# A four-layer graph network on Trainium2: in the last three layers the first block's neighbours past the 15th share one transfer

## The chip, the cores and the metric

The kernel runs on one core of a Trainium2 chip. The core has five engines with a queue each, which they take in order: TensorE (PE in the profile; PEld is its weight load), VectorE (DVE), ScalarE (ACT), GpSimd (POOL) and SyncE (SP). They wait for one another through semaphores. Plain transfers are started from SP's queue, indirect ones (a list of row numbers picks the rows) from POOL's. The metric is the device time of one execution in microseconds; a lower one is better. It is given as the median of ten runs; the profile is of one execution more.

## The reference

4096 nodes with 256 features pass four attention layers over one sparse graph. Each layer normalises, applies a weight matrix, and gives each node a softmax-weighted sum over its neighbours and itself:

```python
# layer 0
h = jnp.maximum(_layernorm(x, axis=-1), 0.0)
x = x + _L0_gnn_ref(h, adj, L0_gnn_W, L0_gnn_a)
# layers 1, 2, 3: the same with _L1_gnn_ref, _L2_gnn_ref, _L3_gnn_ref
...
# L0, and L2 with a bias and without elu: 4 heads, scores from two vectors
e = s_i[:, None, :] + s_j[None, :, :]
e = jax.nn.leaky_relu(e, negative_slope=0.2)
e = jnp.where((adj == 0)[:, :, None], -jnp.inf, e)
alpha = jax.nn.softmax(e, axis=1)
out = jnp.einsum('ijh,jhd->ihd', alpha, Wh).reshape(n, heads * d)
...
# L1: 1 head, sums the nodes rather than their products
att = jax.nn.softmax(e, axis=1)
return h + att @ node
...
# L3: dot products, 4 heads of 64
scores = jnp.einsum('hnd,hmd->hnm', q, k) / np.sqrt(HEAD_DIM)
attn = jax.nn.softmax(scores + mask[None, :, :], axis=-1)
ctx = jnp.einsum('hnm,hmd->hnd', attn, v)
```

The graph is drawn at random and symmetric, with some 8 neighbours a node.

## The kernel before

A first stage (to about 430 us) reads the 4096 x 4096 adjacency, makes a list of at most 23 neighbours for each node, computes layer 0's table and part of its sums, and sorts the nodes by their number of neighbours, most first. Each node's row is then written to its place in that order. A flag checks the lists' limits; when it fails, a dense path runs instead (it doesn't here).

The layers then work on 32 **blocks** of 128 nodes, one node to a partition. As the nodes are sorted, block b needs only `CAPS[b]` columns of neighbours: 23 for block 0, then 14, 13, 12, 12, down to 3 for block 31. A row with fewer neighbours has its list filled with the number n = 4096, the table's one extra row, whose scores are so low that their share is 0. Layers 1 to 3 take the blocks in the order 0, 31, 1, 30, 2, 29 and so on (`ORDER`).

For layer l, each block writes its 128 rows to a table in HBM, `s_tab`. Rows are 264 floats wide in layers 0 and 2, 288 in layer 1 (with the node's own list in the last columns) and 512 (key and value) in layer 3. When the last rows of a table have landed, the next layer starts:

- `layer` goes over the blocks; `fill` issues the transfers ahead of use. One neighbour column of one block is one indirect transfer from POOL (`fetch`, L757): 128 rows, one to a partition, into one **slot** of a ring in SBUF. The ring has 18432 floats a partition: 69 slots in layer 2, 64 in layer 1, 36 in layer 3. A block takes consecutive slots (in layers 2 and 3 one more where its count is odd) and starts over at slot 0 where the end doesn't fit; `fill` stops as long as the slots belong to a block that is not yet done in program order. A transfer into a slot that was used waits, on the chip, for its last reader.
- `scores` makes the scores of a block's columns and of the node itself. In layers 1 and 2 that is one addition over all columns (L918); in layer 3 a product with the node's query and a sum over each head, for 8 columns at a time (L937, L940). `mutual` checks in layer 1 that each neighbour lists the node too (L965 to L973), and ACT takes the neighbours' places in the new order from the rows (L924), so that layers 2 and 3 gather by place. Then come the maximum, the difference and the exponential (L949, L950, L957).
- `weigh` normalises and sums. In layer 1 DVE multiplies and adds column by column (L1010). In layers 2 and 3 DVE multiplies 8 columns at a time by their shares (L1039), and PE adds them up in PSUM, two slots to a product with the identity (L1044); the node's own term is either one of the slots (odd counts) or a product of its own (L1032).
- `settle` adds the sums to x (L1078; in layer 3 L1068 and L1069, into `s_out`, of which there are three), normalises, and `turned`, `times` and `advance` make the next layer's rows (L742, L744, L750, L1091 to L1118). In layer 3 the outputs are stored by indirect transfers from POOL (`send`, L767), between the gathers.

The order of the layers' instructions is the order in which the program is written; each engine takes its own in that order. `reload`, ahead of layer 0, loads the sorted lists (`s_near`) and the rows (`s_rx`). PE's small results go through `pp`, a pool of three PSUM buffers. `verdict` gathers the flags at the end.

Of the kernel before, what the change touches and what calls it, by code (L numbers as in the profile page):

```python
# [19 lines left out]
P = 128  # L20
D = 256
# [20 lines left out]
    8, 8, 8, 7, 7, 7, 7, 6, 6, 6, 6, 5, 5, 5, 4, 3,  # L42
]

MARK = 8192.0
FAR = -1e30
W = 264
# [22 lines left out]


class Sparse:

# [611 lines left out]
    def reload(self):  # L687

        nc, tc, nt, n = self.nc, self.tc, self.nt, self.n
        by_place = self.placed.rearrange("(b p) k -> p b k", p=P)  # L690
        near = self.near = self.big.tile([P, nt, 32], U32, name="s_near")
        for a, b in ((0, 2), (nt - 2, nt), (2, nt - 2)):
            back = nc.sync.dma_start(
                out=near[:, a:b, 0 : TOPK + 1],
                in_=by_place[:, a:b, OWN : OWN + TOPK + 1].bitcast(U32),
            )
            if a == 0:
                for i in self.sent:
                    tc.add_manual_dep(
                        back.ins, i.name,  # L700
                        mybir.DependencyInfo(
                            mybir.DependencyClass.Sync, mybir.DependencyReason.DATA
                        ),
                        reason="every row",
                    )
            for k in {0: [], nt - 2: FIRST[:5], 2: FIRST[5:]}[a]:
                nc.sync.dma_start(out=self.rx[k], in_=self.placed[ts(k, P), 0:OWN])

        self.own_f = self.big.tile([P, nt], F32, name="s_own_f")
        nc.vector.tensor_copy(self.own_f, near[:, :, TOPK])  # L710

        where = self.big.tile([P, nt], F32, name="s_place_of")
        nc.gpsimd.iota(
            where, pattern=[[P, nt]], base=0, channel_multiplier=1,
            allow_small_or_imprecise_dtypes=True,
        )
        nc.vector.tensor_copy(near[:, :, TOPK - 1], where)
        self.away = self.big.tile([P, nt, TOPK], F32, name="s_away")
        nc.vector.tensor_scalar(
            self.away, near[:, :, 0:TOPK], float(n), FAR, ALU.is_ge, ALU.mult  # L720
        )

# [52 lines left out]
    def layers(self):  # L777
        tc, nc, nt = self.tc, self.nc, self.nt
        with ExitStack() as ctx:
            big = self.big = ctx.enter_context(tc.tile_pool(name="s_big", bufs=1))  # L780
            self.pool = ctx.enter_context(tc.tile_pool(name="s_main", bufs=2))
            self.pacc = ctx.enter_context(tc.tile_pool(name="s_pacc", bufs=4, space=PSUM))
            shares = ctx.enter_context(tc.tile_pool(name="s_pe", bufs=1, space=PSUM))
            self.pp = ctx.enter_context(tc.tile_pool(name="s_pp", bufs=3, space=PSUM))

            self.turns = 0
            self.shares = shares.tile([P, IB], F32, name="s_shares")

            rx = big.tile([P, nt, D + WL], F32, name="s_rx")
            self.x = [rx[:, b, 0:D] for b in range(nt)]  # L790
            self.rows = [rx[:, b, D : D + W] for b in range(nt)]
            self.rx = [rx[:, b, 0:OWN] for b in range(nt)]
            self.before = [rx[:, b, OWN - 4 : OWN] for b in range(nt)]
            self.listed = [rx[:, b, D : D + WL] for b in range(nt)]
            self.ring = big.tile([P, RING], F32, name="s_ring")
            self.eself = big.tile([P, nt, 4], F32, name="s_eself")
            self.norms = big.tile([P, 2, nt], F32, name="s_norms")
            self.both = big.tile([P, nt], F32, name="s_both")
            with tc.manual_schedule():
                self.reload()  # L800
                for l in range(4):
                    self.layer(l)
            return self.verdict()

    def slots(self, l, b):
        return max(CAPS[b] - EARLY, 0) if l == 0 else CAPS[b]

    def layer(self, l):

# [9 lines left out]
        def fill(i):  # L819
            nonlocal at  # L820
            while todo and nt - len(todo) <= i + AHEAD:
                j = todo[0]
                K = self.slots(l, j)

                room = K + (K % 2 if l > 1 else 0)
                s = (at if at + room <= slots else 0) if K else 0
                if any(s < e and b < s + room for b, e in held.values()) or (
                    l == 3 and len(held) > 3
                ):
                    return  # L830
                todo.pop(0)
                if l == 3:
                    vs[j] = self.pool.tile([P, D], F32, name=f"s_vself_{j}", tag="vself", bufs=5)
                    nc.sync.dma_start(out=vs[j], in_=self.tab[3][ts(j, P), D:])
                k0 = EARLY if l == 0 else 0
                for k in range(K):
                    at_k = self.near[:, j, k0 + k : k0 + k + 1]
                    self.fetch(ring[:, s + k, :], self.tab[l], at_k)
                held[j] = (s, s + room)
                at = s + room if K else at  # L840

# [29 lines left out]
        for i in range(nt):  # L871
# [3 lines left out]
                settle(c, (0,))  # L875
            norm(d)
            g = ring[:, held[b][0] : held[b][1], :]
            p = self.scores(l, b, self.rows[b], g[:, : self.slots(l, b), :])
            third(e)
            if l == 0:  # L880
                settle(c, (1,))
# [22 lines left out]
    def scores(self, l, b, mine, g):  # L904
# [1 line left out]

        nc, pool = self.nc, self.pool
        H = 1 if l == 1 else 4
        K = self.slots(l, b)
        if K == 0:  # L910
            return None
        e = pool.tile([P, TOPK, H], F32, name=f"s_e_{l}_{b}", tag="e", bufs=3)
# [1 line left out]
        if l < 3:  # L914
            src = mine[:, D + H : D + 2 * H]
            if l > 0:
                nc.vector.tensor_tensor(e[:, K, :], mine[:, D : D + H], src, ALU.add)
            nc.vector.tensor_tensor(  # L918
                e[:, :K, :], g[:, :, D : D + H], src.unsqueeze(1).to_broadcast([P, K, H]), ALU.add
            )  # L920
            if l == 1:
                self.mutual(b, g)

                nc.scalar.copy(self.near[:, b, 0:K], g[:, :, WL - 1])  # L924
            slope = 0.01 if l == 1 else 0.2
            el = ek if l > 0 else ek[:, : K * H]
            nc.vector.scalar_tensor_tensor(el, el, slope, el, ALU.mult, ALU.max)
# [2 lines left out]
        else:  # L930
            q = self.shares[:, IB - D :]
            nc.scalar.copy(q, mine[:, 0:D])
            nc.scalar.copy(e[:, K, :], self.eself[:, b, :])
            for k0 in range(0, K, AT_ONCE):
                m = min(AT_ONCE, K - k0)
                kq = g[:, k0 : k0 + m, 0:D]
                nc.vector.tensor_tensor(  # L937
                    kq, kq, q.unsqueeze(1).to_broadcast([P, m, D]), ALU.mult
                )
                nc.vector.tensor_reduce(  # L940
                    e[:, k0 : k0 + m, :], kq.rearrange("p k (h d) -> p k h d", h=4), AX.X, ALU.add
                )
            nc.vector.tensor_tensor(
                e[:, :K, :], e[:, :K, :],
                self.away[:, b, :K].unsqueeze(2).to_broadcast([P, K, 4]), ALU.add,
            )
        by_head = e[:, : K + 1, :].rearrange("p k h -> p h k")
        top = pool.tile([P, H], F32, name=f"s_m_{l}_{b}", tag="m", bufs=3)
        nc.vector.tensor_reduce(top, by_head, AX.X, ALU.max)  # L949
# [10 lines left out]
    def mutual(self, b, g):  # L960

        nc, pool = self.nc, self.pool
        K = CAPS[b]
        eq = pool.tile([P, CAPS[0], TOPK - 1], BF16, name=f"s_eq_{b}", tag="eq", bufs=1)
        nc.vector.tensor_scalar(  # L965
            eq[:, :K, :], g[:, :, W : WL - 1], self.own_f[:, b : b + 1], None, ALU.is_equal
        )
        has = pool.tile([P, CAPS[0]], F32, name=f"s_has_{b}", tag="has", bufs=1)
        nc.vector.tensor_reduce(has[:, :K], eq[:, :K, :], AX.X, ALU.max)
# [5 lines left out]
    def weigh(self, l, b, me, g, p):  # L975

        nc, pool = self.nc, self.pool
        H = 1 if l == 1 else 4
        K = self.slots(l, b)
        tot = pool.tile([P, H], F32, name=f"s_t_{l}_{b}", tag="t", bufs=3)  # L980
        if K == 0:

# [22 lines left out]
        acc = both[:, 0, :]  # L1005
        self.turns += 1
        if l == 1:
            nc.vector.tensor_scalar(acc, me, p[:, K, :], None, ALU.mult)
            for k in range(K):
                nc.vector.scalar_tensor_tensor(  # L1010
                    acc, g[:, k, 0:D], p[:, k, :], acc, ALU.mult, ALU.add
                )
            return acc
        v0 = 0 if l < 3 else D


        pairs = l > 1
        full = pairs and K % 2 == 0
        if pairs and not full:
            mev = g[:, K, v0 : v0 + D]  # L1020
        else:
            mev = pool.tile([P, D], F32, name=f"s_me_{l}_{b}", tag="me", bufs=4)
        if full:
# [7 lines left out]
        elif full:  # L1031
# [1 line left out]
                both, lhsT=self.ident, rhs=mev.unsqueeze(1).to_broadcast([P, 2, D]),  # L1033
                start=True, stop=False,
            )
        for k0 in range(0, K, AT_ONCE):
            m = min(AT_ONCE, K - k0)
            v = g[:, k0 : k0 + m, v0 : v0 + D].rearrange("p k (h d) -> p k h d", h=H)
            nc.vector.tensor_tensor(  # L1039
                v, v, p[:, k0 : k0 + m, :].unsqueeze(3).to_broadcast([P, m, H, D // H]), ALU.mult  # L1040
# [1 line left out]
            for k in range(k0, k0 + m, 2 if pairs else 1):  # L1042
                if pairs:
                    nc.tensor.matmul(  # L1044
                        both, lhsT=self.ident, rhs=g[:, k : k + 2, v0 : v0 + D],
                        start=(k == 0 and not full), stop=(k + 2 >= K),
                    )
                else:
                    nc.tensor.matmul(  # L1049
                        acc, lhsT=self.ident, rhs=g[:, k, v0 : v0 + D],  # L1050
                        start=False, stop=(k + 1 == K),
                    )
        return both if pairs else acc

    def settle(self, l, b, acc, made):
# [631 lines left out]
```

## Time and profile before

| | us |
|---|---|
| median of 10 runs (1813.22 to 1820.92) | 1816.24 |
| the profiled execution | 1817.75 |
| its span | 1816.0 |
| layer 1, first gather to the next layer's first (642.05 to 1012.56) | 370.5 |
| layer 2 (1012.56 to 1388.4) | 375.8 |
| layer 3 (1388.4 to the span's end) | 427.6 |

Busy shares of the span: DVE 76%, POOL 65%, PE 54% (with matmul ends that are modelled), ACT 23%. POOL issues 924 gathers into the ring (`s_ring<-s_tab,s_near`), 277 in each of layers 1 to 3. A row of the timeline gives the start in us, the duration, the engine, the line, the operation, output and inputs, and in brackets the idle time before it with what ended it. A row of waits gives who waited for whom, the total in us, how often, and the longest. PEclk is the clock granted to TensorE as a share of the full one.

### The profile page before, as it was taken

The numbers are of one execution on the slowest core, as the hardware profiler recorded it, in microseconds if no ns is written. First come the engines' busy times: TensorE is split into PE (matmuls) and PEld (weight loads), VectorE is DVE, ScalarE is ACT, GpSimd is POOL, SyncE is SP. The second block draws the span as 40 slices with busy tenths as digits, with TensorE's granted clock in tenths as the row PEclk, the third lists the DMA queues.
The fourth block names the chain that finished last, engine by engine and source line by source line (L and its number), as shares of the span: only waits on it lengthen the run. The fifth ranks groups of instructions, "written<-read, shape, count | busy, mean of one in ns | idle before, by whom it ended". The sixth has DMA issues, their size and how long they took to land.

```text
span 1816.0 us, 14325 instructions
## 1 busy us (share of the span) xinstructions
PE 975.2 (54%) x2534; PEld 473.0 (26%) x2551; DVE 1383.4 (76%) x3900; ACT 424.5 (23%) x1240; POOL 1184.7 (65%) x1324
## 2 busy tenths in 40 slices
PE   4967787752676602222222067788684354454445
PEld 3623233220454401111111033334332121111112
DVE  6899989951689818888888167888885587887776
ACT  5864434101244401111111012222221000000000
POOL 1067756676666267777776577777773577776774
PEclk9989889875788955555555588899987677677787
DMA  9899877347633144444444344444443577665763
GB/s 323 280 393 361 293 271 254 101 144 235 191 96 95 45 104 124 132 129 133 131 132 112 76 121 133 132 137 131 136 131 120 155 213 209 207 208 180 210 204 109
DMA packets 123017, 312.89 MB, mean 172 GB/s; under 512 B 31236, under 2 KB 49671, under 8 KB 122920
## 3 DMA queue, kind: packets, MB, share of 16 engines
q0 software_dynamic: 68064, 207.46, 40.6%
q1 hardware_dynamic: 54856, 104.44, 16.3%
q14 instruction: 73, 0.60, 0.1%
q8 instruction: 24, 0.39, 0.1%
HBM read 276.80 MB, written 35.00 MB: 172 GB/s over the span
## 4 chain that ended last, share of the span: by engine, by line
DVE 38%; POOL 16%; DMA 15%; issue 14%; PE 14%; ACT 3%; DVEq 0%; SPq 0%; POOLq 0%; another core or an unknown queue 0%; ACTq 0%
DMA s_ring<-s_tab,s_near 10%; POOL s_ring L757 10%; DVE s_acc L1010 7%; PE s_acc L1044 5%; POOL s_g L757 4%; DVE s_cand L485 3%; DVE s_ring L1039 3%; PE s_ps_kv L750 2%; DVE s_g L549 2%; DVE s_ring L937 1%; DVE s_st L571 1%; PE s_ae L558 1%; PE s_acc L1049 1%; DVE s_e L940 1%; DMA out_dram<-s_out,s_near 1%
## 5 line engine op out<-in xcount | busy, mean ns | idle before, releaser
L757 POOL DMA_INDIRECT s_ring<-s_tab,s_near x924 | 883.3, 956 | 348.3 <-issue 185.6
L1044 PE MATMUL s_acc<-s_ring,s_ident 128*128 128x512 f32 x588 | 307.5, 675 | 187.6 <-issue 96.2
L757 POOL DMA_INDIRECT s_g<-s_tab,s_keep x192 | 183.1, 954 | 64.4 <-issue 56.1
L1044 PEld LDWEIGHTS s_acc<-s_ring,s_ident 128*128 128x128 f32 x588 | 125.8, 220 | 362.6 <-issue 241.1
L485 DVE MAX8 s_cand<-s_pt 128x8 f32<-128x256 f32 x512 | 181.4, 415 | 16.3 <-PE s_pt L483 15.7
L1039 DVE TENSOR_TENSOR s_ring<-s_ring,s_shares 128x2048 f32<-128x2048 f32 (+7 forms) x121 | 187.5, 1573 | 0.0
L742 PE MATMUL s_pht<-s_ident,s_h 128*128 128x128 f32 x128 | 34.3, 361 | 249.9 <-ACT s_h L734 249.9
L750 PE MATMUL s_ps<-s_we_l,s_ht 128*128 128x264 f32 x256 | 114.8, 592 | 93.0 <-ACT s_ht L744 93.0
L1010 DVE SCALAR_TENSOR_TENSOR s_acc<-s_ring,s_p,s_acc 128x256 f32<-128x256 f32 x277 | 135.7, 490 | 9.7
L263 ACT ACTIVATE s_low<-s_raw 128x1024 fp8e4<-128x1024 int32 x128 | 134.3, 1051 | 20.4 <-DMA s_raw<-in_adj_dram 18.6
L558 PE MATMUL s_ae<-s_g,s_ident 128*128 128x512 f32 x192 | 114.3, 691 | 38.0 <-DVE s_g L549 37.7
L478 PE MATMUL s_pt<-s_low,s_mark 128*128 128x512 fp8e4 x256 | 107.1, 418 | 34.2 <-DVE s_cand L485 13.8
L750 PE MATMUL s_ps_kv<-s_wkv,s_ht 128*128 128x512 f32 x128 | 83.6, 788 | 67.1 <-ACT s_ht L744 67.1
L577 ACT ACTIVATE s_y<-s_mv,s_eps 128x1 f32<-128x1 f32 x96 | 28.3, 294 | 388.8 <-DVE s_mv L572 388.8
L937 DVE TENSOR_TENSOR s_ring<-s_ring,s_shares 128x2048 f32<-128x2048 f32 (+7 forms) x48 | 81.1, 1690 | 35.3 <-DMA s_ring<-s_tab,s_near 34.7
L957 ACT ACTIVATE s_shares<-s_e 128x32 f32<-128x32 f32 (+8 forms) x87 | 17.6, 202 | 377.5 <-DVE s_e L950 377.5
L918 DVE TENSOR_TENSOR s_e<-s_ring,s_rx 128x8 f32<-128x8 f32 (+12 forms) x87 | 15.8, 181 | 116.1 <-DMA s_ring<-s_tab,s_near 110.8
L483 PE MATMUL s_pt<-s_places,s_stands 128*128 128x512 bf16 x239 | 98.9, 414 | 1.4 <-DVE s_stands L455 1.4
L750 PEld LDWEIGHTS s_ps<-s_we_l,s_ht 128*128 128x128 f32 x256 | 63.9, 276 | 124.1 <-ACT s_ht L744 114.1
L742 PEld LDWEIGHTS s_pht<-s_ident,s_h 128*128 128x128 f32 x128 | 18.0, 172 | 290.9 <-ACT s_h L734 278.8
L940 DVE TENSOR_REDUCE s_e<-s_ring 128x32 f32<-128x2048 f32 (+7 forms) x48 | 81.2, 1692 | 1.6
L502 POOL TENSOR_SCALAR s_ids<-s_top 128x23 f32<-128x23 f32 x32 | 10.1, 314 | 107.5 <-DVE s_top L493 107.1
(195 smaller groups left out, 1692.3 us busy)
## 6 DMA issues: line engine op xcount, KB each, us to landing
s_raw<-in_adj_dram SPq DMA_DIRECT2D x128, 512.0 KB, 7.9
s_ring<-s_tab,s_near POOLq DMA_INDIRECT x924, 3.0
s_rx<-s_placed SPq DMA_DIRECT2D x32, 262.0 KB, 7.3
s_tab<-s_kv SPq DMA_DIRECT2D x32, 256.0 KB, 2.9
s_tab<-s_keep SPq DMA_DIRECT2D x8, 528.0 KB, 6.8
s_tab<-s_rx SPq DMA_DIRECT2D x32, 132.0 KB, 2.4
s_keep<-in_x_dram SPq DMA_DIRECT2D x8, 512.0 KB, 8.7
s_vself<-s_tab SPq DMA_DIRECT2D x32, 128.0 KB, 3.0
```

Source lines behind the costliest of these rows:

```text
L263: nc.scalar.activation(low[r][:, ts(h, n // 4)], raw.pop(q), AF.Copy, saturate=False, accum_out=self.sums[:, r, h : h + 1],)
L478: nc.tensor.matmul(pt, lhsT=self.mark, rhs=lo[:, ts(g, IB)], start=True, stop=False)
L483: nc.tensor.matmul(pt, lhsT=self.stands[:, g, :], rhs=self.places, start=False, stop=True)
L485: nc.vector.max(out=cand[:, g * (IB // CH) + k, :], in_=pt[:, ts(k, CH)])
L558: nc.tensor.matmul(acc, lhsT=self.ident, rhs=g[:, :, k, 0:D], start=False, stop=(k == E - 1))
L750: self.nc.tensor.matmul(ps[:, :width], lhsT=ht[:, c, :], rhs=w[:, c, :], start=(c == 0), stop=(c == KC - 1),)
L757: return self.nc.gpsimd.indirect_dma_start(out=out, out_offset=None, in_=table[:, :], in_offset=bass.IndirectOffsetOnAxis(ap=idx, axis=0),)
L937: nc.vector.tensor_tensor(kq, kq, q.unsqueeze(1).to_broadcast([P, m, D]), ALU.mult)
L940: nc.vector.tensor_reduce(e[:, k0 : k0 + m, :], kq.rearrange("p k (h d) -> p k h d", h=4), AX.X, ALU.add)
L1010: nc.vector.scalar_tensor_tensor(acc, g[:, k, 0:D], p[:, k, :], acc, ALU.mult, ALU.add)
L1039: nc.vector.tensor_tensor(v, v, p[:, k0 : k0 + m, :].unsqueeze(3).to_broadcast([P, m, H, D // H]), ALU.mult)
L1044: nc.tensor.matmul(both, lhsT=self.ident, rhs=g[:, k : k + 2, v0 : v0 + D], start=(k == 0 and not full), stop=(k + 2 >= K),)
```

## The change

Block 0's lists are cut to 15 columns (`KEPT`) in layers 1 to 3. The entries past the 15th of all its rows, real neighbours only, are numbered through as **edges**, and one transfer fetches them, one edge to a partition. It goes to slot 16 of the block's room, which is now 17 slots in each of the three layers (before: 23 in layer 1, 24 in 2 and 3). The last column of the lists, and with it the number of columns in the softmax, stays 23.

`share_place`, called at the end of `reload`, makes two 0/1 matrices of 128 x 128 (row to edge, edge to row), the list of the edges' rows, and a check that there are at most 128. `more_scores` brings each edge its node's score or query by a product, computes the edge's score, and brings it back to its row and column by another. `more_rows` brings each edge its share, multiplies the fetched row by it, and a last product with `to_row` adds the edges' rows to their nodes: in layers 2 and 3 into the block's sum in PSUM, in layer 1 into a buffer that is added to x.

```diff
+KEPT = 15
+MORE = CAPS[0] - KEPT
...
+    def share_place(self):
+        near = self.near[:, 0, KEPT : CAPS[0]]
+        nc.vector.tensor_scalar(some, near, float(n), None, ALU.is_lt)
+        for k, by in ((0, (self.ones, self.below)), (1, (self.ones,))):
+            for lhsT in by:
+                nc.tensor.matmul(
+                    ps[:, ts(k, MORE)], lhsT=lhsT, rhs=some, start=(lhsT is self.ones),
+                    stop=(lhsT is by[-1]),
+                )
...
+        nc.vector.scalar_tensor_tensor(self.to_edge, i, many, past, ALU.is_lt, ALU.mult)
+        nc.tensor.transpose(pt[:, 0:P], self.to_edge, self.ident)
+        nc.scalar.copy(self.to_row, pt[:, 0:P])
+        nc.tensor.matmul(pe[:, : MORE + 4], lhsT=self.to_edge, rhs=of, start=True, stop=True)
...
+        nc.vector.scalar_tensor_tensor(self.far, self.none, float(n), row, ALU.mult, ALU.add)
+
+    def more_scores(self, l, mine, ge, e):
+        if l < 3:
+            nc.tensor.matmul(
+                ps[:, 0:H], lhsT=self.to_edge, rhs=mine[:, D + H : D + 2 * H], start=True,
+                stop=True,
+            )
+            nc.vector.tensor_tensor(s, ge[:, D : D + H], ps[:, 0:H], ALU.add)
+        else:
+            nc.tensor.matmul(ps[:, 0:D], lhsT=self.to_edge, rhs=mine[:, 0:D], start=True, stop=True)
+            nc.vector.tensor_tensor(ge[:, 0:D], ge[:, 0:D], ps[:, 0:D], ALU.mult)
+            nc.vector.tensor_reduce(
+                s, ge[:, 0:D].rearrange("p (h d) -> p h d", h=H), AX.X, ALU.add
+            )
...
+        nc.vector.tensor_tensor(
+            to, self.which.unsqueeze(2).to_broadcast([P, MORE, H]),
+            s.unsqueeze(1).to_broadcast([P, MORE, H]), ALU.mult,
+        )
...
+        nc.tensor.matmul(back, lhsT=self.to_row, rhs=to, start=True, stop=True)
+        nc.vector.tensor_tensor(
+            e[:, KEPT : CAPS[0], :], back,
+            self.away[:, 0, KEPT : CAPS[0]].unsqueeze(2).to_broadcast([P, MORE, H]), ALU.add,
+        )
+
+    def more_rows(self, l, p, ge):
+        nc.scalar.copy(own, p[:, KEPT : CAPS[0], :])
+        nc.tensor.matmul(ps, lhsT=self.to_edge, rhs=own, start=True, stop=True)
+        nc.vector.tensor_tensor(
+            to, ps, which.unsqueeze(2).to_broadcast([P, MORE, H]), ALU.mult
+        )
+        nc.vector.tensor_reduce(s, to.rearrange("p j h -> p h j"), AX.X, ALU.add)
+        nc.vector.tensor_tensor(v, v, s.unsqueeze(2).to_broadcast([P, H, D // H]), ALU.mult)
+        return ge[:, v0 : v0 + D]
...
     def slots(self, l, b):
-        return max(CAPS[b] - EARLY, 0) if l == 0 else CAPS[b]
+        return max(CAPS[b] - EARLY, 0) if l == 0 else min(CAPS[b], KEPT)
...
-                room = K + (K % 2 if l > 1 else 0)
+                more = l > 0 and j == 0
+                room = KEPT + 2 if more else K + (K % 2 if l > 1 else 0)
...
                     self.fetch(ring[:, s + k, :], self.tab[l], at_k)
+                if more:
+                    self.fetch(ring[:, s + KEPT + 1, :], self.tab[l], self.far)
...
+            if more:
+                self.more_scores(l, mine, g[:, KEPT + 1, :], e)
...
         if l == 1:
+            if more:
+                rows = self.more_rows(l, p, g[:, KEPT + 1, :])
+                by_edge = self.pp.tile([P, IB], F32, tag="ps", name="s_by_edge")[:, 0:D]
+                nc.tensor.matmul(by_edge, lhsT=self.to_row, rhs=rows, start=True, stop=True)
             nc.vector.tensor_scalar(acc, me, p[:, K, :], None, ALU.mult)
...
+            if more:
+                nc.vector.tensor_tensor(self.x[b], self.x[b], by_edge, ALU.add)
             return acc
...
+        if more:
+            rows = self.more_rows(l, p, g[:, KEPT + 1, :])
+            nc.tensor.matmul(
+                both, lhsT=self.to_row, rhs=rows.unsqueeze(1).to_broadcast([P, 2, D]),
+                start=False, stop=True,
+            )
```

In layer 1 `more_scores` also does the list check for the edges (four small instructions on DVE) and takes the edges' places into `self.far` (ACT), by which layers 2 and 3 fetch. In layers 2 and 3 `more_rows` comes after the last columns' L1039, and its small product after their L1044 in PE's queue. `share_place` has 18 instructions on DVE, three iotas on POOL, five products on PE and a copy on ACT.

## The prediction

> **What bounds the kernel now.** I read the stage windows first, then each engine's waits inside a stage, then the timeline at the layer starts. Layers are l = 0 to 3, times are span microseconds. The windows' columns are PE, PEld, DVE, ACT, POOL busy, granted clock, DMA share, GB/s.
>
> ```profile
> 638.00:676.00 38.00, 0.00 (x0) 0.00 (x0) 0.45 (x4) 0.48 (x3) 26.74 (x28) 0.50 0.49 100
> 676.00:996.00 320.00, 84.46 (x180) 43.90 (x180) 278.14 (x951) 50.87 (x185) 238.17 (x250) 0.50 0.47 129
> ...
> 1012.00:1046.00 34.00, 0.00 (x0) 0.00 (x0) 0.08 (x1) 0.00 (x0) 25.52 (x27) 0.50 0.51 96
> 1046.00:1364.00 318.00, 247.92 (x599) 119.78 (x600) 257.11 (x750) 76.22 (x262) 239.66 (x251) 0.90 0.48 131
> ```
>
> l = 1 and l = 2 each open with some 35 us in which only POOL works: it issues the 23 gathers of block 0. A gather costs POOL 0.95 us and 0.30 us to the next, a pitch of 1.257 us, and POOL then issues without a gap: 250 in 320 us is 1.27 each. Who is late at the end of a layer is in the timeline:
>
> ```profile
> 669.76 0.95 POOL L757 DMA_INDIRECT s_ring<-s_tab,s_near  x1 [0.30 <-issue]
> 675.85 0.19 DVE L918 TENSOR_TENSOR s_e<-s_ring,s_rx 128x23 f32<-128x23 f32 x1 [37.55 <-DMA s_ring<-s_tab,s_near]
> ...
> 989.15 0.95 POOL L757 DMA_INDIRECT s_ring<-s_tab,s_near  x1 [0.30 <-issue]
> 995.91 0.17 DVE L918 TENSOR_TENSOR s_e<-s_ring,s_rx 128x8 f32<-128x8 f32 x1
> ...
> 1207.86 0.95 POOL L757 DMA_INDIRECT s_ring<-s_tab,s_near  x1 [0.30 <-issue]
> 1211.01 0.20 DVE L918 TENSOR_TENSOR s_e<-s_ring,s_rx 128x40 f32<-128x40 f32 x1 [1.21 <-DMA s_ring<-s_tab,s_near]
> ...
> 1360.89 0.95 POOL L757 DMA_INDIRECT s_ring<-s_tab,s_near  x1 [0.30 <-issue]
> 1364.43 0.19 DVE L918 TENSOR_TENSOR s_e<-s_ring,s_rx 128x32 f32<-128x32 f32 x1 [0.98 <-DMA s_ring<-s_tab,s_near]
> ```
>
> A waiting DVE starts 3.15 us after a block's last gather (1207.86 to 1211.01). In l = 2 it still waits at the last block (3.54): POOL bounds l = 2. In l = 1 it starts 6.76 late and without a wait: after block 0, DVE bounds l = 1, with POOL 3.6 us behind it as the next bound. Block 0 is special: its last gather takes 6.09 us to DVE's start (5.7 in l = 2, 6.3 in l = 3). Of block 0's 128 rows only 46, 21, 9, 7, 2, 0, 0, 0 have a neighbour in columns 16 to 23 (counted from the reference's adjacency); the rest fetch the one pad row. That this makes them late is my reading; the lateness is in the rows.
>
> In l = 3 the scores are taken 8 columns at a time while gathers land, and the ring has only 36 slots of this width:
>
> ```profile
> 1401.07 2.29 DVE L937 TENSOR_TENSOR s_ring<-s_ring,s_shares 128x2048 f32<-128x2048 f32 x1 [10.99 <-DMA s_ring<-s_tab,s_near]
> ...
> 1422.41 2.02 DVE L937 TENSOR_TENSOR s_ring<-s_ring,s_shares 128x1792 f32<-128x1792 f32 x1 [6.50 <-DMA s_ring<-s_tab,s_near]
> ...
> 1431.70 14.62 PE L1044 MATMUL s_acc<-s_ring,s_ident 128*128 128x512 f32 x28 [42.87 <-DVE s_ring L1039]
> ...
> 1434.05 0.95 POOL L757 DMA_INDIRECT s_ring<-s_tab,s_near  x1 [13.24 <-PE s_acc L1044]
> ...
> 1446.58 2.29 DVE L937 TENSOR_TENSOR s_ring<-s_ring,s_shares 128x2048 f32<-128x2048 f32 x1 [1.06 <-DMA s_ring<-s_tab,s_near]
> ```
>
> Blocks 0, 31 and 1 want 24 + 4 + 14 = 42 slots, so block 1 starts over at slot 0 and POOL stands 13.24 us until block 0's first products have read it. From there POOL issues 268 transfers (gathers and output stores) in 343 us with only two gaps over 1 us (3.46 and 2.61), and DVE's largest wait is for stores that POOL issues late:
>
> ```profile
> DVE s_out L1068 <- DMA out_dram<-s_out,s_near: 34.6, 12, 7.9
> ```
>
> So POOL bounds l = 3 as well, after one hole of 13 us.
>
> **l = 1.** POOL: 23 gathers become 16, 7 x 1.257 = 8.8 us. DVE waits for column 15 instead of 23, at 642.05 + 14 x 1.257 + 3.15 = 662.8 instead of 675.85: 13.0 earlier. The shared transfer lands 1.26 later, behind the list check (L965 to L973, some 2 us), so nobody waits. DVE loses 8 multiply-adds (23 took 12.04, so 0.523 each: 4.2) and a third of L965 and L969 (0.4). It gains about ten instructions: eight small ones at a pitch of 0.21 (as L970, L973) and two over 256 columns at 0.42 (as L1078), 2.5 us. And it now stands twice for PE: at "back", and at the shares in more_rows, which go over ACT (0.25). The nearest trip there and back is L734 to L742 to L744 at this layer's clock: ACT done at 695.06, ACT again at 696.01, 0.95 us for two products. Bounds: 0.7 (one such product alone) and 2.6 (the four of L750, 2.13, with their waits); I take 1.2, a small product with weights of its own being nearest to L742. Net: 2.5 + 2.65 - 4.6 = +0.6. DVE could be 12.4 earlier; POOL allows 8.8 plus what the lag can shrink, from its smallest, 6.2 us at block 14, to 3.15: **11.9 us**.
>
> Trainium skill, "DMA: Bandwidth & Descriptors", section "Anatomy of one DMA": a GpSimd transfer takes about 2.0 us plus its bytes over 436 GB/s, whatever rows it reads; an estimate of 2.3 us for these 147 KB. By it DVE would start only 8 x 1.257 = 10.1 us earlier, l = 1 would gain 9.5, and the sum below would be 2.4 us less. The trace disagrees: 6.09 against 3.15 for the same bytes.
>
> **l = 2.** Gathers: **8.8 us**. DVE starts 12.6 earlier, and loses 2.1 (L1039 over 15 columns is 2.29 + 2.02, not 6.41). It pays 0.6 and 1.2 in more_scores. In more_rows it stands behind PE, which takes its queue in order: 16 product instructions (28 took 13.84; five at 0.85, then 0.43) are 9.0 us, 2.0 of it under the second L1039, so 7.0 of wait, then 0.7 for the small product and 0.8 of DVE's own. Net +8.2, so DVE is 4.4 ahead of the old trace where POOL is 8.8 ahead. The 4.4 is covered: DVE's old 5.04 us wait for those same products (L1078, block 0) mostly goes, and it waits 24.8 us for gathers later in the layer. Without that cover l = 2 would gain 4.4.
>
> **l = 3.** The rooms are 17 + 4 + 14 = 35: block 1 fits, and POOL runs through to 1428.7. Block 30 then takes slots 0 to 3 from 1430. Are they read by then? DVE: chunk one as before to 1405.7, chunk two (7 columns, from 1410) to 1414.1, more_scores 2.5, softmax as before, first L1039 done near 1421.7; the products of slots 0 to 3, two cold pairs, near 1425.3. Yes, with 4.7 us to spare. Block 2 takes slots 4 to 16, the last free after more_rows near 1434, wanted at 1450; block 29 wants 18 to 22 from 1452.7, where block 1 (DVE at 1438.5) frees 21 and 22 near 1454, after the three before them are issued. So the wait goes and doesn't come back: 12.9 us (13.24 less the usual 0.30), with 8.8 for the gathers **21.7 us**. DVE is behind POOL for a while: more_rows makes it wait 7 again, block 1 starts at 1438.5 instead of 1446.58, block 30 at 1453.8 (1465.6), block 2 at 1460.6 (1472.4), 11.8 ahead. It recovers the other 9.9 from the 34.6 us that it used to wait for stores.
>
> **share_place.** 18 small DVE instructions at 0.21 and two PE trips: 6.5 us (4 to 12 by the bounds of the trip), ahead of l = 0. DVE later idles 12.42 us there:
>
> ```profile
> 461.80 0.23 DVE L918 TENSOR_TENSOR s_e<-s_ring,s_rx 128x68 f32<-128x68 f32 x1 [12.42 <-DMA s_ring<-s_tab,s_near]
> ```
>
> That hides it; bare, it would cost its 6.5. POOL's three iotas (0.16 for 32 columns, 0.56 for 512) fall into the 1.80 us before its first gather. The verdict's transposes, now issued at 1388, draw on the same three PSUM buffers as the new products and may be pushed into or behind l = 3; their chain is 2.1 us long. I take 0.5 us for all of this (0 to 4).
>
> Trainium skill, "SBUF — State Buffer", section "SBUF: two separate sides": a vector copy in a two-port mode locks GpSimd out of the port through which it writes descriptors. By that rule the new small instructions, some 10 us of them, could hold gathers back, at worst for all of it, and the sum would be 1784. The trace has 924 gathers of 949, 953 and 1199 ns (least, median, most) beside a busy DVE, so I charge nothing.
>
> **Sum.** 11.9 + 8.8 + 21.7 - 0.5 = 41.9 us. Span 1816.0 to 1774.1; this execution took 1817.75 in all, so about 1775.9; the median shown is 1816.24, 1.5 below, which puts it at 1774.3. **1774**, main case 1768 to 1781.
>
> **Rivals.**
> (B) The ring wait moves rather than goes: block 30 or 29 meets slots not yet read. For it: 36 slots, four blocks held. Against: the walk, with 1 to 5 us of room. l = 3 then keeps 8.8: 29 us, **1787**.
> (C) DVE never recovers: trips nearer 2.6, and more_rows' wait at the cold 0.85 throughout. For it: DVE is at 278 of 320 in l = 1. Against: its waits in l = 2 and l = 3. Gains 11.9 + 4.4 + 11.8 = 28: **1788**.
> (D) The openings were hidden anyway: **1816**. Against: 37.55 and 35.8 us of idle DVE, released by the gathers.
> (E) Slower: DVE's in-order stand behind PE in more_rows is what ends each layer, and the earlier start buys nothing. Price: 6.5 + 0.6 + 8.2 + 4.3 (l = 3: 11.0 added, 6.7 removed), 19.6 us, **1836**. It decides once the stand exceeds the 12 to 13 us of earlier start; I count 7.
>
> More than 128 shared edges would send the program down its dense path; the reference's adjacency gives 85.
>
> **Chances.** Main 0.71, B 0.11, C 0.10, D 0.02, E 0.06. B and C make the upper end, 1789; the lower, 1766, is no overhead at all with the two POOL gaps of 3.46 and 2.61 gone too. A difference under 0.2% can't be told from none here; faster 0.92, same 0.02, slower 0.06.
>
> **What would show it.** Right: L918 of l = 1 some 20.7 us after the layer's first gather (33.8 now); no POOL gap over 2 us between l = 3's first and 50th gather; DVE idle about 7 us in more_rows at l = 2 and 3, and DVE's L918 still waiting for gathers at the end of l = 2. Wrong: a POOL gap there, or l = 2's last block starting far over 3.5 us after its gather.

## The result, and the profile after

The changed kernel takes **1773.89 us** (median of 8 runs, 1762.49 to 1775.69) against 1816.52 (28 runs): a ratio of 0.9756, 95% interval 0.9743 to 0.977, or 42.6 us less. Its profiled execution took 1773.45 us, with a span of 1771.7 (before 1817.75 and 1816.0). Seven of the twelve experiment runs fell into two sessions in which every kernel, the one before too (2149.09 and 2177.26 us), took some 18 to 20% longer, for a reason that no run here shows, so times are compared only within a session. From here on l = 1 is measured from its first gather to that of l = 2, and so on; a layer is cut into its **stream** (first to last gather) and its **tail** (from there to the next layer's first gather, or to the end of the span).

| part | predicted gain, us | span before, us | span after, us | gain | stream | tail |
|---|---|---|---|---|---|---|
| all ahead of l = 1 | -0.5 | 642.0 | 644.1 | -2.1 | | |
| l = 1 | 11.9 | 370.5 | 359.4 | 11.1 | 8.8 | 2.3 |
| l = 2 | 8.8 | 375.9 | 365.3 | 10.6 | 8.8 | 1.8 |
| l = 3 | 21.7 | 427.6 | 402.9 | 24.7 | 21.7 | 3.0 |
| sum | 41.9 | 1816.0 | 1771.7 | 44.3 | 39.3 | 7.1 |

The opening of l = 1 in the timeline of the changed kernel (start, duration, engine and line, and in brackets the idle time ahead of it and what ended it):

```profile
663.05 0.95 POOL L894 DMA_INDIRECT s_ring<-s_tab,s_far_more  x1 [0.30 <-issue]
664.31 0.96 POOL L894 DMA_INDIRECT s_ring<-s_tab,s_near  x1 [0.30 <-issue]
665.04 0.18 DVE L1060 TENSOR_TENSOR s_e<-s_ring,s_rx 128x15 f32<-128x15 f32 x1 [24.66 <-DMA s_ring<-s_tab,s_near]
...
668.11 0.17 DVE L835 TENSOR_TENSOR s_e<-s_back,s_away 128x8 f32<-128x8 f32 x1 [0.75 <-PE s_back L834]
...
670.79 0.17 DVE L851 TENSOR_TENSOR s_by<-s_ps_more,s_which 128x8 f32<-128x8 f32 x1 [0.98 <-PE s_ps_more L848]
```

L1060 (L918 before) stands 20.9 us after the layer's first gather at 644.13, where it stood 33.8. The shared transfer went out at 663.05 and no instruction is seen waiting for it. The two trips to TensorE cost VectorE 0.75 and 0.98 us. Late in l = 1 VectorE waits for gathers, which it did not before; the last such wait is at block 14 (its last gather, then VectorE's start):

```profile
952.24 0.96 POOL L894 DMA_INDIRECT s_ring<-s_tab,s_near  x1 [0.30 <-DVE s_acc L1162]
...
956.51 0.17 DVE L1060 TENSOR_TENSOR s_e<-s_ring,s_rx 128x9 f32<-128x9 f32 x1 [1.77 <-DMA s_ring<-s_tab,s_near]
```

VectorE's timeline in l = 2, at the end of block 0 and into the next blocks, and in l = 3 at the end of block 0:

```profile
1040.93 0.19 DVE L851 TENSOR_TENSOR s_by<-s_ps_more,s_half 128x32 f32<-128x32 f32 x1 [7.32 <-PE s_ps_more L848]
1041.82 0.17 DVE L1060 TENSOR_TENSOR s_e<-s_ring,s_rx 128x12 f32<-128x12 f32 x1
...
1068.92 0.24 DVE L1060 TENSOR_TENSOR s_e<-s_ring,s_rx 128x52 f32<-128x52 f32 x1 [3.46 <-DMA s_ring<-s_tab,s_near]
...
1409.97 0.19 DVE L851 TENSOR_TENSOR s_by<-s_ps_more,s_half 128x32 f32<-128x32 f32 x1 [6.93 <-PE s_ps_more L848]
```

There are the two stands behind TensorE, 7.32 and 6.93 us. In l = 2 VectorE waits for gathers again at 1068.92: it has caught up with POOL 28 us after the stand. At the end of l = 2 (block 15's start, the last gather, block 16's start):

```profile
1336.76 0.19 DVE L1060 TENSOR_TENSOR s_e<-s_ring,s_rx 128x32 f32<-128x32 f32 x1 [0.73 <-DMA s_ring<-s_tab,s_near]
...
1343.07 0.95 POOL L894 DMA_INDIRECT s_ring<-s_tab,s_near  x1 [0.30 <-issue]
...
1346.29 0.19 DVE L1060 TENSOR_TENSOR s_e<-s_ring,s_rx 128x32 f32<-128x32 f32 x1
```

VectorE waits for a gather one block before the end, and starts the last block 3.22 us after the last gather (3.54 before): POOL still ends l = 2. POOL's own queue in l = 3, where it used to stand 13.24 us ahead of block 1:

```profile
1391.44 0.96 POOL L894 DMA_INDIRECT s_ring<-s_tab,s_near  x1 [0.30 <-issue]
1392.70 0.95 POOL L894 DMA_INDIRECT s_ring<-s_tab,s_near  x1 [0.30 <-issue]
```

The second line is block 1's first gather. No gap over 2 us follows in it until a store's 2.58 at 1458.

### The profile page after: what moved, and what is told of

Read it like the earlier page. It is cut to its first block, busy times and chain, and to the rows that moved or that the text cites. A ratio compares the mean times of both kernels' runs of the same rounds, so it can differ in the third digit from the quotient of the medians.

```text
span 1771.7 us, 14355 instructions
## 1 busy us (share of the span) xinstructions
PE 978.8 (55%) x2548; PEld 475.2 (27%) x2565; DVE 1377.8 (78%) x3929; ACT 425.4 (24%) x1245; POOL 1165.4 (66%) x1306
## 5 line engine op out<-in xcount | busy, mean ns | idle before, releaser
L894 POOL DMA_INDIRECT s_ring<-s_tab,s_near x900 | 861.2, 957 | 323.2 <-issue 181.1
L1199 PE MATMUL s_acc<-s_ring,s_ident 128*128 128x512 f32 x572 | 301.9, 679 | 113.7 <-issue 92.4
L1199 PEld LDWEIGHTS s_acc<-s_ring,s_ident 128*128 128x128 f32 x572 | 122.0, 220 | 285.2 <-issue 231.5
L490 DVE MAX8 s_cand<-s_pt 128x8 f32<-128x256 f32 x512 | 181.8, 416 | 18.1 <-PE s_pt L488 17.6
L1194 DVE TENSOR_TENSOR s_ring<-s_ring,s_shares 128x2048 f32<-128x2048 f32 (+7 forms) x119 | 183.1, 1561 | 0.0
L879 PE MATMUL s_pht<-s_ident,s_h 128*128 128x128 f32 x128 | 34.6, 363 | 201.8 <-ACT s_h L871 201.8
L1162 DVE SCALAR_TENSOR_TENSOR s_acc<-s_ring,s_p,s_acc 128x256 f32<-128x256 f32 x269 | 131.8, 490 | 9.4
L1103 ACT ACTIVATE s_shares<-s_e 128x32 f32<-128x32 f32 (+8 forms) x87 | 17.6, 202 | 342.4 <-DVE s_e L1096 332.5
L1081 DVE TENSOR_TENSOR s_ring<-s_ring,s_shares 128x2048 f32<-128x2048 f32 (+7 forms) x47 | 78.8, 1676 | 21.2 <-DMA s_ring<-s_tab,s_near 21.2
L1060 DVE TENSOR_TENSOR s_e<-s_ring,s_rx 128x8 f32<-128x8 f32 (+12 forms) x87 | 15.9, 182 | 89.5 <-DMA s_ring<-s_tab,s_near 85.7
```

Of the source, the lines that this page charges most:

```text
L490: nc.vector.max(out=cand[:, g * (IB // CH) + k, :], in_=pt[:, ts(k, CH)])
L894: return self.nc.gpsimd.indirect_dma_start(out=out, out_offset=None, in_=table[:, :], in_offset=bass.IndirectOffsetOnAxis(ap=idx, axis=0),)
L1081: nc.vector.tensor_tensor(kq, kq, q.unsqueeze(1).to_broadcast([P, m, D]), ALU.mult)
L1162: nc.vector.scalar_tensor_tensor(acc, g[:, k, 0:D], p[:, k, :], acc, ALU.mult, ALU.add)
L1194: nc.vector.tensor_tensor(v, v, p[:, k0 : k0 + m, :].unsqueeze(3).to_broadcast([P, m, H, D // H]), ALU.mult)
L1199: nc.tensor.matmul(both, lhsT=self.ident, rhs=g[:, k : k + 2, v0 : v0 + D], start=(k == 0 and not full), stop=(k + 2 >= G and not more),)
```

## The experiments

**The changed kernel again.**

> The changed kernel itself, beside the others on one chip: 1773.9 us, as its first runs. For the trace: if the 1.8 and 3.0 us by which the stretches after the last gather of l = 2 and l = 3 came out shorter than before belong to the change, they are 25.7 and 24.8 us again; if they hang on how TensorE's clock falls in that profile, they wander by 1 to 3 us.

2125.62 us against 2149.09, ratio 0.9895 (0.9876 to 0.9914): in that session the change earns 23.5 us, not 42.6, and why is open. The question about the tails is answered by the kernels of the other sessions, one profile of each. The table has each tail, the clock granted to TensorE in it, and for l = 3 the time and the clock of the last eight product instructions (the ends of products are modelled, those of the tails are not).

| kernel | l = 2's tail, us | its clock | l = 3's tail, us | last eight products, us | their clock |
|---|---|---|---|---|---|
| before | 27.5 | 0.93 | 27.8 | 6.6 | 0.55 |
| after | 25.7 | 1.00 | 24.8 | 4.4 | 0.84 |
| block 0 with 24 slots | 26.0 | 0.92 | 24.6 | 4.3 | 0.86 |
| 7 gathers of rows | 26.9 | 0.92 | 27.0 | 6.3 | 0.58 |
| 7 gathers of pads | 26.6 | 0.94 | 26.9 | 5.9 | 0.62 |
| own pad rows, early | 25.4 | 0.97 | 26.8 | 5.6 | 0.65 |
| small product first | 29.7 | 0.83 | 25.7 | 5.3 | 0.70 |

In l = 3 the tail is the longer the lower that clock, in the order of all seven, and time times clock is 3.6 to 3.7 us in each. The kernels that fetch 16 times for block 0 of l = 3 stand in both halves of that order (24.6 to 27.0), and by the modelled ends 2.2 of the 3.0 us in the table of results lie in these eight instructions: the gain in l = 3's tail goes with the clock in the profile, and not with the change. In l = 2 the longest tail has the lowest clock and the two shortest the highest, but the order between is not strict; there the tails wander by 4.3 us, more than the 1.8 in question. l = 1's tail behaves otherwise: 23.4 before, and 20.9 to 21.1 in all six others.

**The ring's layout of before, with the gathers of after.**

```
-                room = KEPT + 2 if more else K + (K % 2 if l > 1 else 0)
+                extra = CAPS[0] - KEPT - 1 if more and l == 3 else 0
+                room = KEPT + 2 + extra if more else K + (K % 2 if l > 1 else 0)
```

> The changed kernel, but block 0 of l = 3 reserves 24 ring slots as before (17 used), so that block 1 starts over at slot 0. POOL then has block 0's and block 31's 20 gathers issued some 25.7 us after the layer's first, at 1394.5, and waits for block 0's first products, which TensorE starts at about 1401.2 and needs 0.85 us for: a hole of some 7.5 us. Theory (POOL's stream sets the length of l = 3, so a hole costs its length): 1781. Rival one (the hole is hidden by VectorE's later waits): 1774. Rival two (the wait comes back in full, 12.9): 1787.

1783.66 us against 1816.09 (ratio 0.9824, 0.9811 to 0.9838): 9.8 more than the changed kernel. POOL's timeline at the place:

```profile
1390.78 0.95 POOL L894 DMA_INDIRECT s_ring<-s_tab,s_near  x1 [0.30 <-issue]
1402.77 0.95 POOL L894 DMA_INDIRECT s_ring<-s_tab,s_near  x1 [11.04 <-PE s_acc L1200]
```

The hole is 11.04 us, where I expected 7.5: I counted 20 gathers ahead of it, there are 19 (block 31 has 3 neighbours), and I set the last at 1394.5, where it is at 1390.78. l = 3 grew from 402.9 to 413.7, by 10.8: the hole less the usual 0.30 is 10.74. So a hole in POOL's stream costs its length, as the 12.9 us of the prediction were priced. Rival one of this run, that VectorE's later waits hide it, is out.

**Seven gathers given back in l = 1 and l = 2**, ahead of block 0's own, once from columns 0 to 6, once from columns 16 to 22:

```
+                for k in range(extra):
+                    at_k = self.near[:, 0, 0 + k : 0 + 1 + k]
+                    self.fetch(ring[:, s + KEPT + 2 + k, :], self.tab[l], at_k)
                 for k in range(K):
```

> The changed kernel, with 7 further gathers ahead of block 0's own in l = 1 and l = 2, into ring slots that nobody reads; they fetch the rows of columns 0 to 6. Theory (what the change bought there is POOL's 7 x 1.257 us): each of the two layers 8.8 us longer, 1791.5. Rival (VectorE or TensorE sets the end there and POOL has room): 1774. VectorE's first instruction of l = 1 comes 20.9 + 8.8 = 29.7 us after the layer's first gather.

> As with the rows of columns 0 to 6, but the 7 gathers fetch columns 16 to 22, which are the one pad row in nearly all partitions. POOL's time is the same: 17.6 us, 1791.5. If gathers of one row by many partitions are slow in themselves and hold up those behind them, block 0's own columns land late, VectorE's first instruction of l = 1 comes 31 to 33 us after the first gather instead of 29.7, and l = 1 is up to 3 us longer: 1791.5 to 1794.5. If the rows read do not matter, 29.7 and 1791.5.

1791.62 us (ratio 0.9847, 0.9822 to 0.9872) and 1790.31 (0.9857, 0.9842 to 0.9872), 17.7 and 16.4 over the changed kernel; 14 x 1.257 = 17.6. The streams are back at 347.6 and 349.2 us with rows, and at 347.1 and 348.1 with pads (347.1 and 348.3 in the kernel before): what l = 1 and l = 2 gained in them is the time of seven gathers in POOL's queue. VectorE's first instruction of l = 1, with rows and then with pads:

```profile
670.14 0.18 DVE L1064 TENSOR_TENSOR s_e<-s_ring,s_rx 128x15 f32<-128x15 f32 x1 [33.35 <-DMA s_ring<-s_tab,s_near]
```

```profile
671.69 0.18 DVE L1064 TENSOR_TENSOR s_e<-s_ring,s_rx 128x15 f32<-128x15 f32 x1 [33.34 <-DMA s_ring<-s_tab,s_near]
```

The layers' first gathers are at 640.50 and 642.07, so both come 29.6 us after. Gathers of the pad row put in front of a block delay nobody behind them.

**A pad row for each partition**, in the kernel before. The tables grow by 127 rows, and block 0's list is mended once:

```
+        nc.vector.tensor_scalar(
+            pads, near[:, 0, 0 : CAPS[0]], float(n), where[:, 0:1], ALU.is_ge, ALU.mult
+        )
+        nc.vector.tensor_tensor(
+            near[:, 0, 0 : CAPS[0]], near[:, 0, 0 : CAPS[0]], pads, ALU.add
+        )
```

> The kernel before, with one change: each partition of block 0 fetches a pad row of its own (row n + p) where all fetched row n. Theory (many partitions reading one row makes the last columns land late): VectorE starts block 0 some 3.1 us after its last gather in l = 1, 2 and 3, where it took 6.1, 5.7 and 6.3; l = 1 ends 2.9 us earlier, since VectorE bounds it, l = 2 not at all, since POOL does, and in l = 3 the wait for ring slots shrinks by some 3 us, so 1810.7 against 1816.5. Rival (23 gathers issued in one run pile up in the queue, whatever rows they read): the 6 us stay and the time stays 1816.5.

> The kernel before with a pad row for each partition, on another chip. In the first profile VectorE started block 0 of l = 1 and l = 2 3.1 and 2.8 us after its last gather (6.1 and 5.7 before), so the landing is settled; the time is open. Theory (l = 1 is VectorE's, l = 3 has the ring wait behind it): 1810.7 against 1816. Rival (covered later in each layer): 1816.

2158.85 us against 2149.09 (ratio 1.0054, 1.0033 to 1.0075), and in the other session 2183.65 against 2177.26 (1.004, 1.0024 to 1.0056): slower. The landing did what the theory said: in the first of the two profiles VectorE starts block 0 of l = 1 and l = 2 3.1 and 2.8 us after the last gather. The edit itself stood in the way: it rewrites the list that l = 0's first gather reads, and stood behind the load of all lists, so that this gather came 16.6 us after the last row was placed (5.5 before). So the mending was moved right behind the load of block 0's list:

> The kernel before with a pad row for each partition of block 0, the list of rows mended right behind its load. In the earlier form the mending stood behind the load of all lists, and the first gather of l = 0 came 16.6 us after the last row was placed instead of 5.5, which cost some 11 us and hid what the landing bought. Now the first gather comes about 6.5 us after, and the time is the sum of l = 1 and l = 3 as worked out before, less that 1 us: theory 1811.5 where the kernel before takes 1816 (ratio 0.9972). Rival (the earlier landing is covered later in each layer): no change or 1 us slower, ratio 1.0000 to 1.0005.

1804.64 us against 1817.5, ratio 0.9929 (0.9904 to 0.9954): 12.9 less, almost three times the 4.5 that I expected. The last gather of block 0 in l = 0 in the kernel before (VectorE started at 461.80):

```profile
450.15 0.95 POOL L757 DMA_INDIRECT s_ring<-s_tab,s_near  x1 [0.30 <-issue]
```

The last gather of block 0 and VectorE's start in l = 0, VectorE's start in l = 1, and the wait for ring slots in l = 3, in this kernel:

```profile
453.88 0.95 POOL L768 DMA_INDIRECT s_ring<-s_tab,s_near  x1 [0.31 <-issue]
...
459.43 0.23 DVE L929 TENSOR_TENSOR s_e<-s_ring,s_rx 128x68 f32<-128x68 f32 x1 [10.00 <-DMA s_ring<-s_tab,s_near]
...
666.57 0.19 DVE L929 TENSOR_TENSOR s_e<-s_ring,s_rx 128x23 f32<-128x23 f32 x1 [34.55 <-DMA s_ring<-s_tab,s_near]
...
1421.34 0.95 POOL L768 DMA_INDIRECT s_ring<-s_tab,s_near  x1 [10.86 <-PE s_acc L1055]
```

In l = 1 VectorE starts 3.1 us after the gather at 663.5, and the layer is 2.3 shorter (368.2), all of it in the tail. l = 2 gains 1.8, none of it in its stream. l = 3 gains 2.8, of which 1.8 are in the stream: POOL waits 10.86 us for block 0's slots and not 13.24, 2.4 less where I expected 3. The rest is in l = 0, which I had left out: there block 0's 17 columns hold the same pads, and VectorE starts 5.5 us after the last gather instead of 11.6. From the issue of the last row's placing to l = 1's first gather is 208.5 us here and 217.6 before: 9.1 less. Of these, 6.1 are the landing; the other 3 were not traced, and l = 0 wanders by as much from kernel to kernel (209.3 to 212.3 us from its first gather to l = 1's in the other six, 202.4 here).

**The small product ahead of the others**, so that VectorE does not stand behind TensorE. more_rows is cut in two, and its first half (the copy of the shares and `s_ps_more`) is issued earlier:

```
         v0 = 0 if l < 3 else D
+        if more:
+            ps = self.more_shares(l, p)
...
-            rows = self.more_rows(l, p, g[:, KEPT + 1, :])
+            rows = self.more_rows(l, ps, g[:, KEPT + 1, :])
```

> In l = 2 and l = 3 the small product of more_rows is issued ahead of the 16 instructions of products, so VectorE no longer stands 7.3 and 6.9 us behind TensorE. Theory (POOL's gathers end these layers and VectorE's delay is covered by its later waits for gathers): the wait in more_rows falls under 1 us, VectorE waits some 6 us more for gathers within the next blocks, and the time stays within 2 us of the changed kernel, 1772 to 1774. Rival (VectorE's stand is what ends the layers, or it never recovers): 6 us less in each of the two layers, 1762.

> The same kernel as in the first comparison (the small product of more_rows issued ahead of the 16 instructions of products in l = 2 and l = 3), on another chip, since all kernels, the one before too, took 18% longer on the first. Theory (covered): within 2 us of the changed kernel's 1773.9. Rival (VectorE's stand ends the layers): 1762.

> Once more the small product of more_rows ahead of the 16 instructions of products in l = 2 and l = 3; so far it stood against kernels that all took 18% longer, VectorE's wait there fell to 1 us or less, and the time was the changed kernel's (2125.7 against 2125.6). Where the kernel before takes about 1816 us: theory (VectorE's stand is covered by its later waits for gathers) 1772 to 1774, with VectorE waiting for gathers again from l = 2's second block on; rival (the stand ends the layers) 1762.

In the two longer sessions 2125.73 us, where the changed kernel took 2125.62, and 2145.13 against 2177.26 of before (ratio 0.9868, 0.9836 to 0.99). Where the kernel before takes 1817.5: **1771.22** (ratio 0.9741, 0.972 to 0.9762); the interval covers the changed kernel's 0.9756. VectorE's timeline in l = 2:

```profile
1031.11 0.18 DVE L856 TENSOR_TENSOR s_by<-s_ps_more,s_half 128x32 f32<-128x32 f32 x1
1031.98 0.16 DVE L1065 TENSOR_TENSOR s_e<-s_ring,s_rx 128x12 f32<-128x12 f32 x1
1044.69 0.22 DVE L1065 TENSOR_TENSOR s_e<-s_ring,s_rx 128x56 f32<-128x56 f32 x1 [2.59 <-DMA s_ring<-s_tab,s_near]
```

The 7.32 us are gone (no idle time ahead of L856), block 31 starts 8.6 us after its last gather instead of 15.7, and VectorE then waits for gathers already at block 1, the third in order, at 1044.69. The 7 us were taken from one wait and given to another; the streams of l = 2 and l = 3 are 340.0 and 378.9 us (339.5 and 378.1 in the changed kernel). The rival's 1762 is out. Whether it is worth its 2.7 us of median can't be told from these runs.

**share_place four times over.**

```
+        for _ in range(4):
+            self.share_place_once(i, own, num)
```

> share_place's products and VectorE instructions run four times over (POOL's iotas once), same tiles. One pass took 4.5 us, and VectorE still idled 7.65 us ahead of block 0 of l = 0. Theory (the pass is hidden until that idle time is used up): three more passes are 13.4 us, less 7.65 leaves 5.8 on the path: 1779.7. Rival one (every pass is on the path): 1787. Rival two (all of it is hidden): 1774.

> share_place four times over, on another chip. Theory (hidden until the 7.65 us of idle time are used up): 5.8 us on the path, 1779.7. Rival one (all on the path): 1787. Rival two (all hidden): 1774.

Both runs fell into the longer sessions: 2140.67 us, 15.0 over the changed kernel there, and 2161.73, 16.6 over the kernel with the small product first. In those sessions the two kernels that they are held against have only 0.24 us of idle time ahead of block 0 of l = 0, so there was no cover to use up, and the three further passes cost 5.0 to 5.5 us each: the theory of this run was not put to the test. That a pass is hidden where the cover exists is read from the changed kernel's own trace:

```profile
463.36 0.23 DVE L1060 TENSOR_TENSOR s_e<-s_ring,s_rx 128x68 f32<-128x68 f32 x1 [7.65 <-DMA s_ring<-s_tab,s_near]
```

VectorE's wait is 7.65 us where it was 12.42, and the row starts 31.5 us after the layer's first gather (31.8 before); from that gather to l = 1's first there are 212.3 us (212.1 before). How many passes that cover hides wasn't tried.

## Why the prediction was right, point by point

The forecast of 1774 us met 1773.89, and its mechanism held: POOL's stream of gathers sets the lengths of the last three layers. The closeness of the sum is partly luck, since its errors cancel: 0.8 too much in l = 1, 1.8 and 3.0 too little in the tails of l = 2 and l = 3, and 1.6 too little loss ahead of l = 1 make the 2.4 between 41.9 and the profiled pair's 44.3. The medians lie 42.6 apart, 0.7 from the sum.

- **l = 1, 11.9 against 11.1.** The stream gave its 8.8. The other 3.1 was taken from VectorE's lag behind a block's last gather, which should fall from 6.2 to 3.15 at block 14. VectorE does wait for gathers there, so POOL bounds l = 1 up to that block as said, but it starts 4.27 us after the last gather (952.24 to 956.51) and not 3.15. The 3.15 was read at block 8 of l = 2; block 14 there had 4.24 in the kernel before (1330.54 to 1334.78). At the last block the lag is 4.5 (982.41 to L1060 at 986.9; 6.76 before), and the tail gave 2.3. Own pad rows alone shorten l = 1 by the same 2.3, with all 23 gathers in place: this term comes from the pads leaving the end of block 0's row, and not from fewer gathers. The trip at "back" was put at 1.2 and is 0.75.
- **The pad row** was my reading of 6.09 us where other blocks took 3.15. It is shown now: with the same gathers and bytes but rows of their own, 3.1. (The 3.15 is from l = 2, whose rows have 1056 bytes and not l = 1's 1152; block 0 took 5.7 there.) The Trainium skill, "DMA: Bandwidth & Descriptors", section "Anatomy of one DMA", gives one transfer a fixed time and a time for its bytes, and no term for the rows that it reads; these runs, with 17 to 23 gathers issued one behind another, show one, of 3 us in l = 1 and 6 in l = 0.
- **l = 2, 8.8.** The stream gave 8.8, and the seven gathers given back took it away again. The net loss of VectorE, with a stand of 7.0 (measured 7.32), was called covered; taking the stand away moved nothing that could be measured, and VectorE waits for gathers to the end of the layer.
- **l = 3, 21.7.** The stream gave 21.7. The wait went and didn't come back, and giving it back cost its length. Block 1 started at 1416.69, with the layer begun 19.6 us earlier: 2.2 us sooner than the walk said. Where VectorE then made up the rest was mis-sized: the prediction took 9.9 us from its waits for stores, and these fell from 34.6 to 29.7 only; after block 1's start its waits for gathers fell by 7.7 (11.6 to 3.9) and those for products by 2.2 (5.9 to 3.7).
- **share_place and verdict, 0.5.** share_place took 4.5 us of VectorE (put at 6.5), hidden as said; the price without cover was 5.0 to 5.5 in the longer sessions. The verdict's reductions ran at 1410.3 to 1413.6 inside block 31 of l = 3, where VectorE is behind POOL for a while anyway. Of the 2.1 us that l = 1 began later, 1.9 were there when the last row's placing was issued (424.44 and 426.39), ahead of anything that the change touches.
- **The rivals.** B (the wait moves) is answered by POOL's queue, C (VectorE never recovers) by VectorE's waits for gathers late in l = 1 and l = 2, E (its stand ends each layer) by the small product first, D (hidden anyway) by the gathers given back. For E the point from which it decides was a stand beyond 12 to 13 us; it was 7.

No step of the sum failed; the sizes that were off are the lag of l = 1 (2.3 for 3.1), the source of VectorE's recovery in l = 3, and the tails of l = 2 and l = 3, which the sum took as fixed and which wander by 3 to 4 us from kernel to kernel, in l = 3 with the clock granted to TensorE.

What the change left lying: l = 0 still fetches the pad row in block 0's 17 gathers, and its row starts 31.5 us after the first gather, 26.1 in the kernel with pad rows of its own. The two together were not run.

## What to carry to other kernels

Where one engine issues a long run of small transfers at a fixed pitch, count the issues and the holes of that queue: both cost their length, and waits of other engines that are swallowed by it cost nothing until they outlast it. A stand of 7 us of an engine that later waits for the queue was not worth removing here. Before a difference in a layer's tail is put down to a change, look at the clock granted there. Padding that sends many partitions to one row is no free filler: give each its own, and when you mend a list, look at who is waiting to read it.

## What the runs showed of the hardware

- **Many reads of one row land late.** The last pad gathers of block 0 kept VectorE 6.1 us in l = 1 and 11.6 in l = 0, where other stores and loads run beside them; with rows of their own 3.1 and 5.5. Gathers of other rows issued behind them in l = 1 were not held up (29.6 us with either).
- **A gather's issue costs POOL the same whatever the width of its rows.** From block 0's first gather to its last in the kernel before, the pitch is 1.26 us in l = 1 (rows of 1152 bytes), 1.26 in l = 2 (1056 bytes) and 1.26 in l = 3 (2048 bytes).
- **l = 3's tail follows the clock granted to TensorE.** With 0.55 granted at the last eight product instructions the profile gives them 6.6 us (modelled ends), and the tail, whose end is not modelled, is 27.8; with 0.86 they are 4.3 and 24.6. The five kernels between lie in the same order.
